# A two-layer graph network on one core: a new order of the opening's tables and loads, and layer-2 scores kept in PSUM

## The chip, the cores and the metric

The program runs on one core of a Trainium2 chip. The metric is the device time of one execution in microseconds (us). The profile names the engines PE (TensorE, matmul), PEld (its weight load), DVE (VectorE), ACT (ScalarE), POOL (GpSimd) and SP (SyncE); DMAs are issued from the queues of SP (SPq), ACT (ACTq) and POOL (POOLq).

## The reference, cut to what matters

There are 12,500 nodes with 64 features and 200,000 edges sorted by destination `dst`; `src` is random.

```python
# layer 1 (batch is all zero, so u[batch] is the row u[0] for every node)
msg = relu(concat([x[dst], x[src], edge_attr_32, u[0]]) @ W1 + b1)
agg = segment_sum(msg, dst)
x1  = layernorm(x + relu(concat([x, agg, u[0]]) @ W2 + b2))
# layer 2: one score per edge, a softmax over the edges of each destination
Z   = einsum('ni,rio->nro', x1, fc_weight)
z_s, z_d = Z[src, etype], Z[dst, etype]
e   = relu(sum(concat([z_s, z_d]) * attn_weight[etype, :, 0]))
m   = segment_max(e, dst);  ex = exp(e - m[dst])
out = layernorm(x1 + segment_sum(ex / segment_sum(ex, dst)[dst] * z_s, dst))
```

## The kernel before

**Edges.** Edges are cut into chunks of 128, four chunks into a run, two runs (8 chunks) into a group: 1563 chunks, 196 groups. Since `dst` is sorted, the destinations of a run fit a window of `W` = 96 nodes. Each layer runs over the groups as a software pipeline: every group is a Python generator (`sum0` in layer 1, `sum1` in layer 2), every tile of 125 nodes another (`finish0`, `finish1`), and the order of the instructions on each engine is the order in which the loops call `group(i)` and `node(i)` under a manual schedule.

**Gathers.** The rows of the sources are fetched by `gather` (L83 to L86), one indirect DMA per chunk, issued by POOL: 8 per group, 1563 per layer. Its offsets lie in SBUF (`src_h`, `src_i`, `row_i`). In layer 1 the rows go to `bg` tiles, of which there are 12, so group g+12 waits until group g's tile has been used. In layer 2 they go to `zg` tiles, of which there are 5.

**The opening.** `W1` splits by its input rows, so the products of all nodes with it are made once: `b_tab` holds x @ W1[sources' rows], `a_tab` holds x @ W1[destinations' rows] plus a common row `c1`. `tables(k)` makes one fifth of both (2500 nodes): 20 matmuls of a 64x125 slice of `xa` (x transposed) against the 64x128 `w1x`, so that sources and destinations come side by side; ACT copies one half to `b_s`, DVE adds `c1` to the other half in `a_s`. SP stores each `b_s` as it is made; ACT stores the five `a_s` after the last. Between the tables DVE makes run data from `dg`: `low` (each run's lowest node), `dr` (destinations less `low`, stored to `rel_tab`), `count`, `at`, and from them the rows `base_row` and `slot_row`, which SP, DVE and ACT read with register loads.

The first `GX` = 6 groups don't wait for `b_tab`: their 48 gathers fetch rows of `x` itself, and PE turns these rows and multiplies them by `w1x` (L385, L395). The gather of group 6 is the first that needs all of `b_tab` and `src_i`. PE begins the first group when `row` has been loaded from `rel_tab`; `row` lies in memory that the opening's tiles leave free, so it also waits for their stores.

**Completion of DMAs.** Direct DMAs of SP and ACT take eight completion semaphores in turn, in program order. A DMA therefore waits at its queue until the one that had its semaphore before it has landed, and what stands behind it in that queue waits too.

**Layer 2.** `psc` is one PSUM bank kept for the whole program. Its first 128 columns hold a row of numbers, `iota`, of which 96 are used; the rest is scratch. `sum1` makes the score `e` of each edge with small DVE instructions (L611 to L617), spreads it over the window by multiplying it with the one-hot `oh` (L625, twice, into `oe` and into `psc`), takes the maxima per node (L627 to L629, then PE and DVE), and goes on to the exponentials on ACT (L674, L676) and the sums on PE (L680). `finish1` normalises the finished nodes; `scale1` scales and stores four tiles at a time, and for each store SP first loads the tile's node number into a register (`n0_of(ENG.SP)`, L724).

```python
for to, i in ((oe, slice(0, half)), (other, slice(half, KS))):
    nc.vector.tensor_mul(to, by_run[:, :, i, :], es[:, :, i].unsqueeze(3).to_broadcast([EC, n, half, W]))
```

Of the kernel before, what the change touches and what calls it, by code (L numbers as in the profile page):

```python
# [29 lines left out]
F32 = mybir.dt.float32  # L30
BF16 = mybir.dt.bfloat16
I32 = mybir.dt.int32
# [7 lines left out]
P = 125  # L40
# [13 lines left out]
NWIN = (N + W - 1) // W  # L54
GX = 6
FIRST = 90
NSL = NG - FIRST
NPT, JT = 5, 20
NQ1 = 4
# [6 lines left out]
def gnn_kernel(ctx: ExitStack, tc, x, xT, src, dstp, dst, et, eaT, u, W1, b1, W2, b2, fc, aw, out):  # L66
# [35 lines left out]
    with (  # L102
# [9 lines left out]
        nc.sync.dma_start(src_h, src[:, :GX * K])  # L112
        dg = pre.tile([NQ, RQ, RE], I32, name="dg")
        nc.sync.dma_start(dg, dst.rearrange("(q r) e -> q r e", r=RQ))
        w1x = consts.tile([D, 2, D], F32, name="w1x")
# [5 lines left out]
        c1 = consts.tile([P, D], F32, name="c1")  # L121
        nc.scalar.dma_start(c1, b1.partition_broadcast(P))
        w2u = consts.tile([DE, D], F32, name="w2u")
        nc.scalar.dma_start(w2u, W2[2 * D:, :])
        c2 = consts.tile([P, D], F32, name="c2")
        nc.scalar.dma_start(c2, b2.partition_broadcast(P))
        w1e = consts.tile([128, D], F32, name="w1e")
        nc.scalar.dma_start(w1e[W:, :], W1[2 * D:2 * D + DE, :])
        for k in range(NPT):
            (nc.scalar if k % 2 else nc.sync).dma_start(xa[:D, part[k]], xT[:, part[k]])  # L130

# [41 lines left out]
        for t in up:  # L173
            nc.vector.memset(t, float(P))
        minus_p = consts.tile([128, 1], F32, name="minus_p")
        nc.vector.tensor_scalar_mul(minus_p, iota_p, -1.0)
        psc = fixed.tile([128, 512], F32, name="psc")

        nc.vector.tensor_copy(psc[:, :128], iota)
        iota_n, iota_r = psc[:EC, :W], psc[:EC, :NR]  # L180


        def common(c, wu):
            ps = pps.tile([P, 4, 2 * D], F32, tag="ab", name="ps_c")
            nc.tensor.matmul(ps[:, 0, :D], u0.to_broadcast([DE, P]), wu, start=True, stop=True)
            nc.vector.tensor_add(c, c, ps[:, 0, :D])

        common(c1, w1u)
        common(c2, w2u)

# [10 lines left out]

        dst_i = keep.tile([EC, NC], I32, name="dst_i")
        a_s = []

        def tables(k):
            b_k = pre.tile([P, JT, D], F32, name="b_s", bufs=3)
            a_k = pre.tile([P, JT, D], F32, name="a_s", bufs=NPT)
            for q in range(JT // 4):
                ps = pps.tile([P, 4, 2 * D], F32, tag="ab", name="ps_ab")
                for i in range(4):  # L210
                    j = k * NP + q * 4 + i
                    nc.tensor.matmul(ps[:, i, :], xa[:D, j:j + JT * (P - 1) + 1:JT], w1x, start=True, stop=True)
                mine = slice(q * 4, q * 4 + 4)
                nc.scalar.copy(b_k[:, mine, :], ps[:, :, D:])
                nc.vector.tensor_add(a_k[:, mine, :], ps[:, :, :D], c1[:, None, :].to_broadcast([P, 4, D]))
            nc.sync.dma_start(b_tab[part[k], :].rearrange("(p j) d -> p j d", j=JT), b_k)
            a_s.append(a_k)
            sums = slice(k * NP, (k + 1) * NP if k < NPT - 1 else N + W)
            nc.scalar.copy(xa[D:, sums], none[D:].to_broadcast([D, sums.stop - sums.start]))

        tables(0)

# [8 lines left out]
        nc.sync.dma_start(bases[1].rearrange("(q r) -> q r", r=RQ), count)  # L231
        tables(1)
        nc.scalar.dma_start(dst_i, dstp)

# [6 lines left out]
        nc.sync.dma_start(bases[2].rearrange("(q r) -> q r", r=RQ), at)  # L241
        tables(2)
        both = pre.tile([1, 3, NRUN], F32, name="both")
        nc.sync.dma_start(both, bases.rearrange("(o s) r -> o s r", o=1))
        tables(3)
        tables(4)
        for k in range(NPT):
            nc.scalar.dma_start(a_tab[part[k], :].rearrange("(p j) d -> p j d", j=JT), a_s[k])
        nc.scalar.dma_start(a_tab[N:, :], zero)


        src_i = keep.tile([EC, NC], I32, name="src_i")
        nc.sync.dma_start(src_i, src)

        aws = []
        for j in range(4):
            t = npool.tile([128, S, D], F32, name=f"aw{j}")
            nc.scalar.copy(t[W:, :, :], w1e[W:, None, :].to_broadcast([DE, S, D]))
            aws.append(t)
        nc.scalar.dma_start(d_tab[N:, :], zero_q)  # L260
        et_i = keep.tile([EC, NC], I32, name="et_i")
        nc.scalar.dma_start(et_i, et)
        w2x = consts.tile([2 * D, D], F32, name="w2x")
        nc.scalar.dma_start(w2x, W2[0:2 * D, :])
        fcw = consts.tile([D, NR, D], F32, name="fcw")
        nc.scalar.dma_start(fcw, fc.rearrange("r i o -> i r o"))
        wsd = consts.tile([D, 2, NR], F32, name="wsd")
        awb = consts.tile([D, 2, NR, D], F32, name="awb")
        for s in range(2):
            nc.scalar.dma_start(awb[:, s, :, :], aw[:, s * D:(s + 1) * D].partition_broadcast(D))  # L270
        rel = keep.tile([EC, NC], F32, name="rel")
# [247 lines left out]
    with (  # L519
# [5 lines left out]
        for i in range(-3, NG + 2):  # L525
# [9 lines left out]
            group(i + 3)  # L535
            if i == 2 * GX:
                later()
# [41 lines left out]

    def sum1(work, psum, n, chunks, idx, rel_of, et_of, row_of, wins_of):  # L580
        row = row_of()
# [34 lines left out]
        nc.vector.tensor_add(e, e, zg[:, :, D])  # L616
        nc.vector.scalar_tensor_tensor(e, e, 0.0, pq[:, :, 3 * NR], OP.max, OP.mult)  # L617


        half = KS // 2  # L620
        by_run, es = oh.rearrange("p (s i) w -> p s i w", s=n), e.rearrange("p (s i) -> p s i", s=n)
        oe = work.tile([EC, n, half, W], F32, name="oe")
# [47 lines left out]
        nc.vector.tensor_reduce(em, pm, AX.X, OP.add)  # L670
        nc.vector.tensor_sub(e, e, em)
        nc.scalar.activation(factor, d, AF.Exp)  # L672
        wz = work.tile([EC, n * KS, C], F32, name="wz")
        nc.scalar.activation(wz[:, :, D], e, AF.Exp)  # L674
        for k in range(n * KS):
# [11 lines left out]

    def finish1(work, psum, n0_of, y_of):

        n0 = n0_of(ENG.SP)  # L690
        xn = work.tile([P, D], F32, name="xn1", bufs=5)
        nc.sync.dma_start(xn, x1_tab[ds(n0, P), :])
        yield
        n0 = n0_of(ENG.Activation)
        own = work.tile([C, P], F32, name="own")
        nc.scalar.copy(own, acc[:, ds(n0, P)])
        yield
        pl = psum.tile([P, C], F32, name="pl")
        nc.tensor.transpose(pl, own, ident[:C, :C])
        yield  # L700
        y, mv = y_of()
        den = work.tile([P, 1], F32, name="den")

        nc.vector.tensor_scalar_max(den, pl[:, D:], 1e-30)
        nc.vector.reciprocal(den, den)
        nc.vector.scalar_tensor_tensor(y, pl[:, :D], den, xn, OP.mult, OP.add)
        st = work.tile([P, nc.vector.BN_STATS_DIM], F32, name="ln_st")
        nc.vector.bn_stats(out=st, in_=y)
        nc.vector.bn_aggr(out=mv, in_=st)

    def scale1(work, n0s_of, y, mv):
        n = len(n0s_of)
        v = work.tile([P, n], F32, name="ln_v")
# [7 lines left out]
        yield  # L721
        for j, n0_of in enumerate(n0s_of):
            nc.scalar.activation(y[:, j, :], y[:, j, :], AF.Identity, bias=shift[:, j:j + 1], scale=v[:, j:j + 1])  # L723
            nc.sync.dma_start(out[ds(n0_of(ENG.SP), P), :], y[:, j, :])  # L724

    with (
# [4 lines left out]
        psum = Banks(pool, pq=2, pb=2)  # L731
        groups, slots, ys, scales = {}, {}, {}, {}

# [7 lines left out]
        for i in range(-3, NG + 4):  # L741
            g = i + 3
            if g < NG:
                n, chunks, c = span(g)
                groups[g] = sum1(work, psum, n, chunks, row_i[:, c], rel[:, c], et_i[:, c],
                                 row_load(work, g), wins_load(g))
            if FIRST <= i < NG:
                slots[i] = finish1(work, psum, slot(i), lambda i=i: y_of(i))
            group(i + 3)
# [26 lines left out]
            if FIRST <= i - 3 < NG and (at == NQ1 - 1 or i - 3 == NG - 1):  # L776
                scales = {q: scale1(work, [slot(j) for j in range(i - 3 - at, i - 2)], *ys[q])}
                next(scales[q])

    with (  # L780
# [11 lines left out]
        def node1(at):  # L792
            y = work.tile([P, 1, D], F32, name="y1")
            mv = work.tile([P, 1, nc.vector.BN_AGGR_DIM], F32, name="ln_mv")
            all_of(finish1(work, psum, lambda engine: at, lambda: (y[:, 0, :], mv[:, 0, :])))
            all_of(scale1(work, [lambda engine: at], y, mv))

# [43 lines left out]
```

## Time and profile before

| | |
|---|---|
| time, median of 3 runs | 4028.84 us (4027.72 to 4029.41) |
| the profiled execution's own time | 4035.53 us |
| its span in the profile | 4033.8 us |
| busy: POOL | 2998.9 us (74%) |
| busy: PE / DVE / ACT | 2966.9 / 2436.6 / 1451.8 us (74 / 60 / 36%) |
| mean granted clock of TensorE | 0.591 |
| first and last gather of layer 1 | 2.88 and 1977.9 us |
| first and last gather of layer 2 | 2002.55 and 3995.6 us |

The span is the time from the first to the last instruction on the chip. A busy share is the time inside instructions; the pause that POOL needs between two gathers is not counted as busy, so POOL's 74% is not a sign of a free quarter. Where an idle stretch stands behind an instruction in square brackets, it gives the time and the event that the profile holds to have ended it.

### The profile page before, as it was taken

The numbers are of one execution on the slowest core, as the hardware profiler recorded it, in microseconds if no ns is written. First come the engines' busy times: TensorE is split into PE (matmuls) and PEld (weight loads), VectorE is DVE, ScalarE is ACT, GpSimd is POOL, SyncE is SP. The second block draws the span as 40 slices with busy tenths as digits, with TensorE's granted clock in tenths as the row PEclk, the third lists the DMA queues.
The fourth block names the chain that finished last, engine by engine and source line by source line (L and its number), as shares of the span: only waits on it lengthen the run. The fifth ranks groups of instructions, "written<-read, shape, count | busy, mean of one in ns | idle before, by whom it ended". The sixth has DMA issues, their size and how long they took to land. (4 is left out here: it accounts for less than half of the span.)

```text
span 4033.8 us, 63353 instructions
## 1 busy us (share of the span) xinstructions
PE 2966.9 (74%) x16445; PEld 2302.5 (57%) x16446; DVE 2436.6 (60%) x8111; ACT 1451.8 (36%) x3714; POOL 2998.9 (74%) x3140
## 2 busy tenths in 40 slices
PE   4977776668999989899666666556666666666664
PEld 4766665557776766667544444444455555555553
DVE  3144433334555555555477777777777787777776
ACT  2100000001111111111265555555556666666665
POOL 5777777777777777777577777777777777777774
PEclk9876655555656565565655556666665555555556
DMA  5222222222333333333221111111122222222221
GB/s 153 50 52 52 51 45 45 45 45 63 77 76 82 78 78 78 78 80 77 63 29 28 28 28 28 28 28 29 29 32 35 35 35 35 35 34 36 34 36 25
DMA packets 292631, 201.38 MB, mean 50 GB/s; under 512 B 213810, under 2 KB 213940, under 8 KB 291841
## 3 DMA queue, kind: packets, MB, share of 16 engines
q0 software_dynamic: 100032, 103.43, 16.2%
q1 hardware_dynamic: 188580, 87.14, 8.6%
q10 hardware_dynamic: 3646, 6.66, 0.6%
q8 instruction: 133, 2.18, 0.2%
q14 instruction: 240, 1.96, 0.2%
HBM read 155.12 MB, written 41.84 MB: 49 GB/s over the span
## 5 line engine op out<-in xcount | busy, mean ns | idle before, releaser
L84 POOL DMA_INDIRECT zg<-z_tab,row_i x1563 | 1518.2, 971 | 499.6 <-issue 422.7
L84 POOL DMA_INDIRECT bg<-b_tab,src_i x1515 | 1430.9, 945 | 482.8 <-issue 425.2
L408 PE MATMUL pa<-oh,msg 128*64 128x96 f32 x3128 | 534.7, 363 | 212.7 <-ACT msg L403 207.9
L403 ACT ACTIVATE msg<-msg 128x512 f32<-128x512 f32 (+1 forms) x190 | 119.4, 629 | 1534.4 <-DVE msg L402 1526.0
L393 PEld LDWEIGHTS pm<-aw,cb 128*128 128x128 f32 x3128 | 558.3, 275 | 128.0 <-issue 123.4
L408 PEld LDWEIGHTS pa<-oh,msg 128*64 128x64 f32 x3128 | 478.4, 221 | 233.5 <-ACT msg L403 223.7
L393 PE MATMUL pm<-aw,cb 128*128 128x64 f32 x3128 | 597.5, 367 | 0.0
L680 PE MATMUL pb<-oh,wz 128*65 128x96 f32 x3128 | 548.4, 368 | 16.6 <-ACT wz L676 4.1
L680 PEld LDWEIGHTS pb<-oh,wz 128*65 128x65 f32 x3128 | 493.9, 227 | 73.3 <-ACT wz L676 73.3
L402 DVE TENSOR_TENSOR msg<-pm,bg 128x512 f32<-128x512 f32 (+1 forms) x190 | 131.1, 690 | 567.7 <-DMA bg<-b_tab,src_i 412.2
L676 ACT ACTIVATE wz<-zg,wz 128x64 f32<-128x64 f32 x1564 | 394.7, 335 | 6.4
L347 DVE TENSOR_TENSOR oh<-psc,rel 128x768 f32<-128x768 f32 x392 | 370.6, 945 | 11.1 <-DMA row<-rel_tab 8.3
L634 PE MATMUL pt<-ident,t 128*96 128x128 f32 x391 | 123.4, 419 | 339.5 <-DVE mq L420 336.5
L594 ACT ACTIVATE off<-ps_row,minus_p 96x512 bf16<-96x512 f32 x391 | 265.8, 680 | 261.6 <-PE ps_row L593 261.6
L593 PE MATMUL ps_row<-row,ones_row 1*96 1x512 bf16 x391 | 209.5, 536 | 192.3 <-ACT off L594 180.0
L414 DVE TENSOR_TENSOR xa<-xa,pa 64x96 f32 x391 | 100.9, 258 | 379.9 <-PE pa L408 372.4
L634 PEld LDWEIGHTS pt<-ident,t 128*96 128x96 f32 x391 | 50.5, 184 | 429.8 <-issue 405.7
L641 PE MATMUL pt<-ident,m 96*65 96x96 f32 x782 | 176.7, 380 | 159.6 <-DVE m L639 159.6
L388 DVE TENSOR_SCALAR cb<-ps_row,iota_p 96x1024 f32<-96x1024 f32 x196 | 246.2, 1256 | 32.2 <-DMA aw<-a_tab 29.9
L641 PEld LDWEIGHTS pt<-ident,m 96*65 96x65 f32 x782 | 119.7, 221 | 176.8 <-DVE m L639 176.8
L341 PE MATMUL ps_row<-row,ones_row 1*96 1x512 bf16 x391 | 183.8, 564 | 39.5 <-DMA fcw<-in_fc 39.5
L597 ACT ACTIVATE ohT<-off 96x1024 bf16<-96x1024 bf16 x196 | 206.6, 1054 | 6.3
(148 smaller groups left out, 3742.7 us busy)
## 6 DMA issues: line engine op xcount, KB each, us to landing
z_tab<-z SPq DMA_DIRECT2D x106, 253.9 KB
zg<-z_tab,row_i POOLq DMA_INDIRECT x1563
cb<-in_eaT SPq DMA_DIRECT2D x195, 128.0 KB
bg<-b_tab,src_i POOLq DMA_INDIRECT x1515
aw<-a_tab SPq DMA_DIRECT2D x391, 24.0 KB
dw<-d_tab SPq DMA_DIRECT2D x391, 4.7 KB
row<-rel_tab SPq DMA_DIRECT2D x390, 2.0 KB
xn<-in_x SPq DMA_DIRECT2D x106, 31.2 KB
```

The lines of the kernel that those rows point to most:

```text
L84: nc.gpsimd.indirect_dma_start(out=to[:, k, :], out_offset=None, in_=table[:, :], in_offset=bass.IndirectOffsetOnAxis(ap=idx[:, k:k + 1], ...
L341: nc.tensor.matmul(ps[:, s, :RE], ones_row, row[:, s, :], start=True, stop=True)
L347: nc.vector.tensor_tensor(oh, iota_n[:, None, :].to_broadcast([EC, n * KS, W]), rel_of.unsqueeze(2).to_broadcast([EC, n * KS, W]), OP.is_e ...
L388: nc.vector.tensor_scalar(cb[:W, :, :], ps_row, iota_p[:W], None, OP.is_equal)
L393: nc.tensor.matmul(pm[:, k, :], cb[:, s, i * EC:(i + 1) * EC], aw_t[:, s, :], start=True, stop=not raw)
L408: nc.tensor.matmul(pa[D:, s, :], msg[:, k, :], oh[:, k, :], start=(i == 0), stop=(i == KS - 1))
L593: nc.tensor.matmul(ps_row[:, :RE], ones_row, row[:, s, :], start=True, stop=True)
L594: nc.scalar.activation(off[:, s, :], ps_row[:, :RE], AF.Abs, bias=minus_p[:W])
L597: nc.scalar.activation(ohT, off, AF.Relu, bias=1.0, scale=-1.0)
L641: nc.tensor.matmul(rows[:, s, :], m[:, s:s + 1].to_broadcast([W, C]), ident[:W, :W], start=True, stop=True)
L676: nc.scalar.activation(wz[:, k, :D], zg[:, k, :D], AF.Copy, scale=wz[:, k, D:])
L680: nc.tensor.matmul(sums[:, s, :], wz[:, k, :], oh[:, k, :], start=(i == 0), stop=(i == KS - 1))
```

## The change

It has four parts.

1. **Scores.** The score of layer 2 is written to 8 columns of `psc` (columns 96 to 111, two places by the group's parity) and no longer to the SBUF tile `e`; the two multiplications of L625 and the subtraction of L671 read it there. `psc` keeps 96 columns of `iota` instead of 128.
2. **Opening.** `tables` is split: `sources(k)` for all five parts first, each 20 matmuls against the 64 source columns of `w1x`, then `destinations(k)` for all five. A PSUM tile now holds five products of 64 columns instead of four of 128. All stores of both tables are issued on SP, each as its part is made. `b_s` has 5 buffers and `a_s` 3. The parts of `xa` are loaded before the weights of `W2`, `w1e`, `dst_i` and `src_i`, which go to SP's queue; parts 0, 1 and 3 come on ACT's queue and 2 and 4 on SP's. `dst_i` and `src_i` are loaded ahead of the tables. The zero rows of `a_tab` and `d_tab` are stored early. `xa`'s lower half is cleared in one instruction at the end. The loads of `et_i`, `w2x`, `fcw` and `awb` are issued by ACT one per round of layer 1's loop, from round 2 on, and `later()`, which uses them, runs in round 20 instead of 12.
3. **Groups of x.** `GX` is 5: 40 gathers fetch rows of `x`, and the gather of group 5 is the first that needs `b_tab`.
4. **Stores of the result.** SP keeps each tile's node number in a register from `finish1` on, and `scale1` uses it, so the 106 register loads of L724 are gone.

```diff
-GX = 6
+GX = 5
-NPT, JT = 5, 20
+NPT, JT, JQ = 5, 20, 5
...
+        dg = pre.tile([NQ, RQ, RE], I32, name="dg")
+        nc.sync.dma_start(dg, dst.rearrange("(q r) e -> q r e", r=RQ))
+        for k in range(NPT):
+            (nc.sync if k in (2, 4) else nc.scalar).dma_start(xa[:D, part[k]], xT[:, part[k]])
         w2u = consts.tile([DE, D], F32, name="w2u")
-        nc.scalar.dma_start(w2u, W2[2 * D:, :])
+        nc.sync.dma_start(w2u, W2[2 * D:, :])
...
-        for k in range(NPT):
-            (nc.scalar if k % 2 else nc.sync).dma_start(xa[:D, part[k]], xT[:, part[k]])
+        nc.sync.dma_start(dst_i, dstp)
+        src_i = keep.tile([EC, NC], I32, name="src_i")
+        nc.sync.dma_start(src_i, src)
...
+        nc.sync.dma_start(a_tab[N:, :], zero)
+        nc.sync.dma_start(d_tab[N:, :], zero_q)
...
-        nc.vector.tensor_copy(psc[:, :128], iota)
+        nc.vector.tensor_copy(psc[:, :W], iota[:, :W])
...
-        def tables(k):
...
+        def products(k, side):
+            for q in range(JT // JQ):
+                ps = pps.tile([P, JQ, D], F32, tag="ab", name="ps_ab")
+                for i in range(JQ):
+                    j = k * NP + q * JQ + i
+                    nc.tensor.matmul(ps[:, i, :], xa[:D, j:j + JT * (P - 1) + 1:JT], w1x[:, side, :],
+                                     start=True, stop=True)
+                yield slice(q * JQ, (q + 1) * JQ), ps
+
+        def sources(k):
+            b_k = pre.tile([P, JT, D], F32, name="b_s", bufs=NPT)
+            for mine, ps in products(k, 1):
+                nc.scalar.copy(b_k[:, mine, :], ps)
             nc.sync.dma_start(b_tab[part[k], :].rearrange("(p j) d -> p j d", j=JT), b_k)
...
+        def destinations(k):
+            a_k = pre.tile([P, JT, D], F32, name="a_s", bufs=3)
+            for mine, ps in products(k, 0):
+                nc.vector.tensor_add(a_k[:, mine, :], ps, c1[:, None, :].to_broadcast([P, JQ, D]))
+            nc.sync.dma_start(a_tab[part[k], :].rearrange("(p j) d -> p j d", j=JT), a_k)
+
+        for k in range(NPT):
+            sources(k)
...
-        tables(1)
-        nc.scalar.dma_start(dst_i, dstp)
+        destinations(0)
...
-        for k in range(NPT):
-            nc.scalar.dma_start(a_tab[part[k], :].rearrange("(p j) d -> p j d", j=JT), a_s[k])
-        nc.scalar.dma_start(a_tab[N:, :], zero)
+        for k in range(2, NPT):
+            destinations(k)
+        common(c2, w2u)
+        nc.scalar.copy(xa[D:, :], none[D:].to_broadcast([D, N + W]))
...
-            if i == 2 * GX:
+            if i >= 2 and loads:
+                nc.scalar.dma_start(*loads.pop(0))
+            if i == 20:
                 later()
...
-        nc.vector.scalar_tensor_tensor(e, e, 0.0, pq[:, :, 3 * NR], OP.max, OP.mult)
+        score = psc[:EC, W + odd * K:W + odd * K + n * KS]
+        nc.vector.scalar_tensor_tensor(score, e, 0.0, pq[:, :, 3 * NR], OP.max, OP.mult)
...
-        by_run, es = oh.rearrange("p (s i) w -> p s i w", s=n), e.rearrange("p (s i) -> p s i", s=n)
+        by_run, es = oh.rearrange("p (s i) w -> p s i w", s=n), score.rearrange("p (s i) -> p s i", s=n)
...
-        nc.vector.tensor_sub(e, e, em)
+        nc.vector.tensor_sub(em, score, em)
...
-            nc.sync.dma_start(out[ds(n0_of(ENG.SP), P), :], y[:, j, :])
+            nc.sync.dma_start(out[ds(n0, P), :], y[:, j, :])
```

More of the change, by code (lines that the diff above doesn't have):

```diff
@@ L112, in gnn_kernel @@
         nc.sync.dma_start(src_h, src[:, :GX * K])
-        dg = pre.tile([NQ, RQ, RE], I32, name="dg")
-        nc.sync.dma_start(dg, dst.rearrange("(q r) e -> q r e", r=RQ))
         w1x = consts.tile([D, 2, D], F32, name="w1x")
@@ L122, in gnn_kernel @@
         nc.scalar.dma_start(c1, b1.partition_broadcast(P))
+        dg = pre.tile([NQ, RQ, RE], I32, name="dg")
+        nc.sync.dma_start(dg, dst.rearrange("(q r) e -> q r e", r=RQ))
+        for k in range(NPT):
+            (nc.sync if k in (2, 4) else nc.scalar).dma_start(xa[:D, part[k]], xT[:, part[k]])
         w2u = consts.tile([DE, D], F32, name="w2u")
-        nc.scalar.dma_start(w2u, W2[2 * D:, :])
+        nc.sync.dma_start(w2u, W2[2 * D:, :])
         c2 = consts.tile([P, D], F32, name="c2")
-        nc.scalar.dma_start(c2, b2.partition_broadcast(P))
+        nc.sync.dma_start(c2, b2.partition_broadcast(P))
         w1e = consts.tile([128, D], F32, name="w1e")
-        nc.scalar.dma_start(w1e[W:, :], W1[2 * D:2 * D + DE, :])
-        for k in range(NPT):
-            (nc.scalar if k % 2 else nc.sync).dma_start(xa[:D, part[k]], xT[:, part[k]])
+        nc.sync.dma_start(w1e[W:, :], W1[2 * D:2 * D + DE, :])
+        dst_i = keep.tile([EC, NC], I32, name="dst_i")
+        nc.sync.dma_start(dst_i, dstp)
+        src_i = keep.tile([EC, NC], I32, name="src_i")
+        nc.sync.dma_start(src_i, src)
         ident = consts.tile([128, 128], F32, name="ident")
@@ L177, in gnn_kernel @@
         psc = fixed.tile([128, 512], F32, name="psc")
-        nc.vector.tensor_copy(psc[:, :128], iota)
+        nc.vector.tensor_copy(psc[:, :W], iota[:, :W])
         iota_n, iota_r = psc[:EC, :W], psc[:EC, :NR]
         def common(c, wu):
-            ps = pps.tile([P, 4, 2 * D], F32, tag="ab", name="ps_c")
-            nc.tensor.matmul(ps[:, 0, :D], u0.to_broadcast([DE, P]), wu, start=True, stop=True)
-            nc.vector.tensor_add(c, c, ps[:, 0, :D])
+            ps = pps.tile([P, JQ, D], F32, tag="ab", name="ps_c")
+            nc.tensor.matmul(ps[:, 0, :], u0.to_broadcast([DE, P]), wu, start=True, stop=True)
+            nc.vector.tensor_add(c, c, ps[:, 0, :])
         common(c1, w1u)
-        common(c2, w2u)
         low = pre.tile([NQ, RQ], F32, name="low")
@@ L199, in gnn_kernel @@
         nc.sync.dma_start(rel_tab.rearrange("(q r) e -> q r e", r=RQ), dr)
-        dst_i = keep.tile([EC, NC], I32, name="dst_i")
-        a_s = []
-        def tables(k):
[L206 to L215, printed above, removed]
-            nc.sync.dma_start(b_tab[part[k], :].rearrange("(p j) d -> p j d", j=JT), b_k)
[L217 to L221, printed above, removed]
+        def products(k, side):
[10 more added lines that the diff above has]
+                nc.scalar.copy(b_k[:, mine, :], ps)
+            nc.sync.dma_start(b_tab[part[k], :].rearrange("(p j) d -> p j d", j=JT), b_k)
+        def destinations(k):
[5 more added lines that the diff above has]
+            sources(k)
         high = pre.tile([NQ, RQ], F32, name="high")
@@ L241, in gnn_kernel @@
         nc.sync.dma_start(bases[2].rearrange("(q r) -> q r", r=RQ), at)
-        tables(2)
+        destinations(1)
         both = pre.tile([1, 3, NRUN], F32, name="both")
         nc.sync.dma_start(both, bases.rearrange("(o s) r -> o s r", o=1))
-        tables(3)
-        tables(4)
-        for k in range(NPT):
-            nc.scalar.dma_start(a_tab[part[k], :].rearrange("(p j) d -> p j d", j=JT), a_s[k])
-        nc.scalar.dma_start(a_tab[N:, :], zero)
-        src_i = keep.tile([EC, NC], I32, name="src_i")
-        nc.sync.dma_start(src_i, src)
+        for k in range(2, NPT):
+            destinations(k)
+        common(c2, w2u)
+        nc.scalar.copy(xa[D:, :], none[D:].to_broadcast([D, N + W]))
         aws = []
@@ L259, in gnn_kernel @@
             aws.append(t)
-        nc.scalar.dma_start(d_tab[N:, :], zero_q)
         et_i = keep.tile([EC, NC], I32, name="et_i")
-        nc.scalar.dma_start(et_i, et)
         w2x = consts.tile([2 * D, D], F32, name="w2x")
-        nc.scalar.dma_start(w2x, W2[0:2 * D, :])
         fcw = consts.tile([D, NR, D], F32, name="fcw")
-        nc.scalar.dma_start(fcw, fc.rearrange("r i o -> i r o"))
         wsd = consts.tile([D, 2, NR], F32, name="wsd")
         awb = consts.tile([D, 2, NR, D], F32, name="awb")
-        for s in range(2):
-            nc.scalar.dma_start(awb[:, s, :, :], aw[:, s * D:(s + 1) * D].partition_broadcast(D))
+        loads = [(et_i, et), (w2x, W2[0:2 * D, :]), (fcw, fc.rearrange("r i o -> i r o"))]
+        loads += [(awb[:, s, :, :], aw[:, s * D:(s + 1) * D].partition_broadcast(D)) for s in range(2)]
         rel = keep.tile([EC, NC], F32, name="rel")
@@ L578, in gnn_kernel, with sum1 @@
         nc.scalar.copy(t, none[:C].to_broadcast([C, N + W]))
-    def sum1(work, psum, n, chunks, idx, rel_of, et_of, row_of, wins_of):
+    def sum1(work, psum, n, chunks, idx, rel_of, et_of, row_of, wins_of, odd=0):
         row = row_of()
@@ L670, in sum1 @@
         nc.vector.tensor_reduce(em, pm, AX.X, OP.add)
-        nc.vector.tensor_sub(e, e, em)
+        nc.vector.tensor_sub(em, score, em)
         nc.scalar.activation(factor, d, AF.Exp)
         wz = work.tile([EC, n * KS, C], F32, name="wz")
-        nc.scalar.activation(wz[:, :, D], e, AF.Exp)
+        nc.scalar.activation(wz[:, :, D], em, AF.Exp)
         for k in range(n * KS):
@@ L685, in sum1, with finish1 @@
             nc.vector.tensor_add(mine, mine, sums[:, s, :])
-    def finish1(work, psum, n0_of, y_of):
+    def finish1(work, psum, n0_of, y_of, tell=lambda n0: None):
         n0 = n0_of(ENG.SP)
@@ L692, in finish1 @@
         nc.sync.dma_start(xn, x1_tab[ds(n0, P), :])
+        tell(n0)
         yield
@@ L709, in finish1, with scale1 @@
         nc.vector.bn_aggr(out=mv, in_=st)
-    def scale1(work, n0s_of, y, mv):
-        n = len(n0s_of)
+    def scale1(work, n0s, y, mv):
+        n = len(n0s)
         v = work.tile([P, n], F32, name="ln_v")
@@ L721, in scale1 @@
         yield
-        for j, n0_of in enumerate(n0s_of):
+        for j, n0 in enumerate(n0s):
             nc.scalar.activation(y[:, j, :], y[:, j, :], AF.Identity, bias=shift[:, j:j + 1], scale=v[:, j:j + 1])
-            nc.sync.dma_start(out[ds(n0_of(ENG.SP), P), :], y[:, j, :])
+            nc.sync.dma_start(out[ds(n0, P), :], y[:, j, :])
     with (
@@ L731, in gnn_kernel @@
         psum = Banks(pool, pq=2, pb=2)
-        groups, slots, ys, scales = {}, {}, {}, {}
+        groups, slots, ys, scales, places = {}, {}, {}, {}, {}
         def y_of(i):
@@ L745, in gnn_kernel @@
                 groups[g] = sum1(work, psum, n, chunks, row_i[:, c], rel[:, c], et_i[:, c],
-                                 row_load(work, g), wins_load(g))
+                                 row_load(work, g), wins_load(g), g % 2)
             if FIRST <= i < NG:
-                slots[i] = finish1(work, psum, slot(i), lambda i=i: y_of(i))
+                slots[i] = finish1(work, psum, slot(i), lambda i=i: y_of(i), lambda n0, i=i: places.update({i: n0}))
             group(i + 3)
@@ L776, in gnn_kernel @@
             if FIRST <= i - 3 < NG and (at == NQ1 - 1 or i - 3 == NG - 1):
-                scales = {q: scale1(work, [slot(j) for j in range(i - 3 - at, i - 2)], *ys[q])}
+                scales = {q: scale1(work, [places[j] for j in range(i - 3 - at, i - 2)], *ys[q])}
                 next(scales[q])
@@ L795, in node1 @@
             all_of(finish1(work, psum, lambda engine: at, lambda: (y[:, 0, :], mv[:, 0, :])))
-            all_of(scale1(work, [lambda engine: at], y, mv))
+            all_of(scale1(work, [at], y, mv))
         leftover(more1, node1)
```

## Prediction

> **What bounds the kernel now.** I read the page's busy row first, then POOL's groups and its waits, because POOL's idle time is where a kernel of 3126 gathers shows its limit:
>
> ```profile
> PE 2966.9 (74%) x16445; PEld 2302.5 (57%) x16446; DVE 2436.6 (60%) x8111; ACT 1451.8 (36%) x3714; POOL 2998.9 (74%) x3140
> L84 POOL DMA_INDIRECT zg<-z_tab,row_i x1563 | 1518.2, 971 | 499.6 <-issue 422.7 <-DVE t L628 26.2 <-DMA zg<-z_tab,row_i 22.9
> L84 POOL DMA_INDIRECT bg<-b_tab,src_i x1515 | 1430.9, 945 | 482.8 <-issue 425.2 <-DMA a_tab<-zero 21.4 <-DMA bg<-b_tab,src_i 18.6
> L84 POOL DMA_INDIRECT bg<-in_x,src_h x48 | 47.9, 999 | 15.0 <-issue 14.3 <-DMA src_h<-in_src 0.7
> ```
>
> Busy and idle of the three groups add up to 1518.2 + 499.6 + 1430.9 + 482.8 + 47.9 + 15.0 = 3994.4 us of the 4033.8. POOL is never free: between two gathers it pauses 0.30 us, whatever the name behind the arrow. Two idle stretches alone are longer, one of 21.38 us ahead of the first gather of `b_tab` and one of 23.5 us between the layers. So the time is 3126 gathers of about 0.944 + 0.304 = 1.248 us (3901), plus these two stretches (44), plus gathers that take longer than usual (46), plus 2.9 us ahead and 37 us behind. Only the last four can change.
>
> The tile view and the timeline show the longer gathers: median 944 ns, maximum 1332, and who runs when one starts late:
>
> ```profile
> L84 POOL DMA_INDIRECT zg<-z_tab,row_i x1563: 940/944/1332, 2002.5 to 3995.6; - x196
> 3984.36 0.17 DVE L616 TENSOR_TENSOR e<-e,zg 128x8 f32<-128x8 f32 x1 [1.48 <-DMA zg<-z_tab,row_i]
> 3984.76 0.56 DVE L625 TENSOR_TENSOR oe<-oh,e 128x384 f32<-128x384 f32 x1
> 3985.24 0.56 DVE L625 TENSOR_TENSOR psc<-oh,e 128x384 f32<-128x384 f32 x1
> 3985.42 1.19 POOL L84 DMA_INDIRECT zg<-z_tab,row_i  x1 [0.31 <-issue]
> ```
>
> The opening, and the end, from the timeline:
>
> ```profile
> 11.72 2.29 DVE L198 TENSOR_TENSOR dr<-dg,low 98x2048 bf16<-98x2048 int32 x1
> 11.77 3.06 POOL L84 DMA_INDIRECT bg<-in_x,src_h  x1 [0.30 <-issue]
> 19.17 46.61 PE L212 MATMUL ps_ab<-w1x,xa 64*125 64x128 f32 x200 [9.94 <-DMA xa<-in_xT]
> 25.56 0.36 SPq L196 DMA_DIRECT2D base_b<-bases  x1
> 66.21 10.76 ACTq L248 DMA_DIRECT2D a_tab<-a_s  x4
> 86.52 0.94 POOL L84 DMA_INDIRECT bg<-b_tab,src_i  x1 [21.38 <-DMA a_tab<-zero]
> 105.31 1.05 PE L341 MATMUL ps_row<-row,ones_row 1*96 1x512 bf16 x2 [39.53 <-DMA fcw<-in_fc]
> 4017.08 9.62 SPq L724 DMA_DIRECT2D out<-y  x6
> 4021.08 0.75 ACT L723 ACTIVATE y<-y,ln_shift,ln_v 125x64 f32<-125x64 f32 x2
> ```
>
> The reader is to see that the gather at 86.5 doesn't really wait for `a_tab`: its inputs are `b_tab` and `src_i`, and the last `b_s` store (issued at 66.2) runs beside the `a_tab` stores. In windows, the stores run at 130 GB/s from 30 to 35 us with one queue storing, and at 124 GB/s from 70 to 84 with two: the second queue adds nothing.
>
> **Part 1, scores: -39 us.** The excess of `zg` gathers over 944 ns sums to 1518.2 - 1563 x 0.944 = 42.7 us. Counted over the trace by what DVE runs in a gather's first 250 ns, 194 gathers of `zg` meet L625, and they take 217 ns more on average: 42.2 us. Beside other DVE instructions the excess is nil: 380 gathers meet L347 (one input in PSUM, one in SBUF, 945 ns long), 176 L629, 150 L402, with means within 1 ns of 944. L650 (both inputs in SBUF, 250 ns) adds 6 ns on average. L198 above, both inputs in SBUF, holds a gather for 2.1 us. So what holds a gather is a running DVE instruction with both inputs in SBUF. After the change L625 has `oh` in SBUF and the score in PSUM, like L347.
>
> [...] L649 with one input in PSUM takes 0.24 us, L650 of the same shape with none 0.25. Either way it is covered: DVE waits 253.8 us in 180 groups at L616 for the gather (1.4 us each)[...].
>
> What is late next: gathers after L625 come 0.22 us earlier against DVE's chain, which starts anew at each L616. Shifted by that, about a third of the 390 L650 start within 50 ns of a gather's start, where the trace shows holds of 0 to 54 ns. I count 3 us (bounds 0 and 390 x 83 ns, the longest hold seen at L650, = 32). Sum -42 + 3 = -39.
>
> **Part 2 and 3, the opening: -10 us.** PE: 200 half products of 64 columns instead of 100 of 128. The row above is 233 ns per pass, two passes a matmul; at 64 columns the pair L393 and L395 takes 0.615 us from 115 to 123 us, so 0.31 a matmul and 31 us for each table. Loads move 208 GB/s from 2 to 24 us. Ahead of the tables now stand `dg`, `xa` and 1.6 MB of `dst_i` and `src_i`: 5.6 MB, done by about 30. `xa`'s first part lands at 11 to 16, not 19, so the sources are done at 44 to 48.
>
> But SP's queue is in order. `low` waits for the last part of `xa`, then lands behind `src_i` in the same queue, at about 31.5 (before, landing took from 11.7 to 25.6 behind three parts of `xa`). `base_b` waits for it, and behind `base_b` stand `rel_tab` and all five `b_s` stores. So these start at about 35, and take 625 KB at 115 GB/s (the 130 above less the gathers' 15 to 20) = 5.7 us each: the last lands at about 63 to 64 (bounds 57, if `low` lands at 26, and 68). 40 gathers of x end at 54, so POOL waits about 9.5 us instead of 21.4: a gain of 12, all bounds 7 to 18.
>
> Two things take some back. DVE's `rel` (L272, 1.78 us) and the minima of L304 and L312 (15 short instructions with two SBUF inputs) ran while POOL stood still; now they run at 75 to 91, beside gathers: +2 to 3 us by the hold above. And `bg` has 12 buffers. The gather of group 17 needs group 5 used. The `a_s` stores follow the `b_s` stores in one queue, to 64 + 5 x 5.7 = 92; then `row` and PE start at about 96 (before 105.3). Before, group 6 was used 98.9 us after PE's start, with six groups of x of 11 to 16 us; with five that is 85 to 91, at 181 to 187. POOL comes to group 17 at 63.5 + 12 x 9.98 = 183. This is on the edge (before, the margin was 2.1 us at group 18), worth 0 to 4 us, and partly the same microseconds as the hold. Sum -12 + 2 = -10.
>
> Costed at nothing: the clearing of `xa` in one piece (some 11 us on ACT, covered by the destinations' 31 us on PE), `c2`, and the ACT loads in the loop (ACT is 1 to 2 tenths busy there; a late one would delay `later()`, not needed until group 90). The stretch of 23.5 us between the layers stays: what ends it is the chain behind the last gather.
>
> **Part 4, stores: -4 us.** Inside the loop SP is no bound. At the end it is: the last ACT result is there at 4021.83, but SP, at 1.7 us a store with a register load of 0.53 us and a wait, issues its sixth store at 4026.4, and everything to 4033.8 follows that. Without the loads it follows ACT at about 4022.2: -4 (bounds -1, -5).
>
> **Sum.** -39 - 10 - 4 = -53 on the profiled 4035.53 us gives 3982.5; that execution stood 6.7 above the median of 4028.84, so 3976.
>
> **The rivals.**
> 1. *As above*, 3976 (own range 3968 to 3986), 74%.
> 2. *PE gives it back*: stores run slower in one queue, or PE's slow stretch falls on the groups of x, and POOL stands at group 17 for the 10 us gained and up to 10 more: 3986 to 3996. For it: the margin of 2.1. Against: the 130 GB/s of one queue. 12%.
> 3. *`low` does not get stuck* and the stall vanishes: the whole 21.4, so 3965. Against: the 13.9 us that it was stuck before. 7%.
> 4. *The hold stays*[...]: -10 - 4, so 4015. 4%.
> 5. *Slower*: the hold comes from L625's length[...], and PSUM makes each of the two longer[...]. [...] It decides as soon as a hold grows by over 0.07 us. Against: L649 and L347. 3%.
>
> **The numbers.** Rivals 1 to 4 end over 0.2% (8 us) below 4028.84, which is about what a measurement of this kernel can tell from no change; rival 5 above it. With 1% in between: faster 0.96, same 0.01, slower 0.03. The range 3964 to 3994 takes in rivals 1 and 3 and most of 2.
>
> **What would show it.** POOL's mean for `zg` falls from 971 to 944 to 950 ns; the gather of `b_tab` starts near 64 with a wait of 5 to 14 us ahead of it; PE's first `ps_row` is near 96; a second POOL wait of under 5 us stands near 183; the last store of `out` is issued near the last ACT result. I am wrong if `zg` stays above 960, if the b_tab wait is over 17 us, or if POOL waits over 10 us at group 17.

## The result

The changed kernel takes 4007.29 us (median of 5 runs, 4000.85 to 4011.78) against 4028.84 (5 runs, 4027.72 to 4029.99): a ratio of 0.9946, 95% interval 0.9932 to 0.9961. It is faster by 21.5 us. Forecast were 53 us, and 4007 lies outside the range of 3964 to 3994. The profiled execution took 4007.29 us with a span of 4005.4.

The groups of POOL in the profile after (busy, mean of one, idle before):

```profile
L84 POOL DMA_INDIRECT zg<-z_tab,row_i x1563 | 1477.4, 945 | 499.4 <-issue 414.7 <-DMA zg<-z_tab,row_i 41.2 <-ACT top L657 23.2
L84 POOL DMA_INDIRECT bg<-b_tab,src_i x1523 | 1442.1, 947 | 492.2 <-issue 443.2 <-DMA bg<-b_tab,src_i 23.5 <-DVE msg L405 13.0
L84 POOL DMA_INDIRECT bg<-in_x,src_h x40 | 39.3, 982 | 15.7 <-issue 11.3 <-DMA bg<-in_x,src_h 3.7 <-DMA src_h<-in_src 0.7
```

The tile view (shortest, median and longest gather, first and last start):

```profile
L84 POOL DMA_INDIRECT zg<-z_tab,row_i x1563: 940/945/1028, 2015.0 to 3967.5; - x196
```

Layer 2, from its first to its last gather, fell from 1993.1 to 1952.5 us: -40.6, as forecast (-39). But its first gather starts at 2015.0, not at 2002.5: the opening, forecast to win 10, lost 12.4. And from the last gather to the end are 37.9 us where there were 38.2: -0.3, forecast -4. Together that is the difference of the two spans (4033.8 to 4005.4). The medians differ by less, 21.5, because the profiled execution of the kernel before stood 6.7 above its median and this one does not (its 4007.29 is the median).

The opening in the timeline after, PE, the stores on SP's queue, and POOL:

```profile
18.96 92.17 PE L213 MATMUL ps_ab<-w1x,xa 64*125 64x64 f32 x400 [7.74 <-DMA xa<-in_xT]
30.87 0.34 SPq L202 DMA_DIRECT2D base_b<-bases  x1
31.77 34.12 SPq L221 DMA_DIRECT2D b_tab<-b_s  x5
73.38 0.94 POOL L84 DMA_INDIRECT bg<-b_tab,src_i  x1 [16.19 <-issue]
93.30 18.64 SPq L227 DMA_DIRECT2D a_tab<-a_s  x3
123.47 1.05 PE L344 MATMUL ps_row<-row,ones_row 1*96 1x512 bf16 x2 [11.74 <-issue]
207.07 0.94 POOL L84 DMA_INDIRECT bg<-b_tab,src_i  x1 [12.37 <-DVE msg L405]
```

Nearly the whole loss is seen here. The tables keep PE busy for 92 us, twice as long as before (46.61). `x400` counts two records for each of the 200 fp32 matmuls; each record is called a pass below. So the sources are done at 65, `b_tab` at 73, the destinations at 111, and PE starts its first group at 123.5 where it started at 105.3. POOL stands twice, 16.19 and 12.37 us, where it stood once for 21.38. That is +7.2 of the 12.4. Gathers of `x` that wait for earlier ones (3.7 us in the row of `in_x`, of which some 3 are more than the usual pauses; before, no such wait is listed) and gathers that last longer (the busy time of layer 1's gathers is 1481.4 us, before 1478.8) are the rest.

### The profile page after: what moved, and what is told of

Its sections match the earlier page's. It is cut to its first block, busy times and chain, and to the rows that moved or that the text cites. A ratio compares the mean times of both kernels' runs of the same rounds, so it can differ in the third digit from the quotient of the medians.

```text
span 4005.4 us, 63587 instructions
## 1 busy us (share of the span) xinstructions
PE 2987.8 (75%) x16621; PEld 2323.1 (58%) x16622; DVE 2472.5 (62%) x8107; ACT 1447.4 (36%) x3703; POOL 2960.7 (74%) x3140
## 5 line engine op out<-in xcount | busy, mean ns | idle before, releaser
L84 POOL DMA_INDIRECT zg<-z_tab,row_i x1563 | 1477.4, 945 | 499.4 <-issue 414.7
L406 ACT ACTIVATE msg<-msg 128x512 f32<-128x512 f32 x191 | 120.0, 628 | 1548.6 <-DVE msg L405 1531.7
L396 PEld LDWEIGHTS pm<-aw,cb 128*128 128x128 f32 x3128 | 548.8, 271 | 126.4 <-issue 122.6
L396 PE MATMUL pm<-aw,cb 128*128 128x64 f32 x3128 | 586.8, 362 | 0.0
L405 DVE TENSOR_TENSOR msg<-pm,bg 128x512 f32<-128x512 f32 x191 | 131.7, 690 | 579.5 <-DMA bg<-b_tab,src_i 432.8
```

The lines of the kernel that those rows point to most:

```text
L84: nc.gpsimd.indirect_dma_start(out=to[:, k, :], out_offset=None, in_=table[:, :], in_offset=bass.IndirectOffsetOnAxis(ap=idx[:, k:k + 1], ...
L396: nc.tensor.matmul(pm[:, k, :], cb[:, s, i * EC:(i + 1) * EC], aw_t[:, s, :], start=True, stop=not raw)
```

## The experiments

| kernel | us | ratio to the kernel before | 95% interval |
|---|---|---|---|
| changed kernel | 4007.3 | 0.9946 | 0.9932 to 0.9961 |
| e1, scores and stores | 4000.1 | 0.9922 | 0.9905 to 0.9938 |
| e1c, scores | 3994.0 | 0.9897 | 0.9882 to 0.9912 |
| e2, opening and 5 groups of x | 4044.0 | 1.0026 | 1.0015 to 1.0038 |
| e3, weights side by side | 4003.9 | 0.9923 | 0.9907 to 0.9940 |
| e4, 16 buffers of `bg` | 3998.5 | 0.9917 | 0.9900 to 0.9933 |
| v2b, tables of 128 columns | 3993.0 | 0.9892 | 0.9877 to 0.9907 |
| e5b, 6 groups of x, 16 buffers | 3980.8 | 0.9861 | 0.9846 to 0.9876 |
| v1b, 128 columns, 7 groups, 16 buffers | 3976.1 | 0.9851 | 0.9837 to 0.9864 |

The runs were made on several chips, so ratios are compared, not times (the kernel before took 4031.6 us beside e1 to e4 and 4036.1 beside e1c, v2b, e5b and v1b). Even ratios carry some 10 us from one chip to the next: e1c, v2b, e5b and v1b, all on one chip, each came out about 10 us below what e1 or the changed kernel on other chips led to expect. Differences of that size are therefore read within one chip, or from the traces. e0, e7, e8 and e9 are single executions. The kernels of v2b, v1b and e5b also ran on one more chip, on which they took 5398 to 5468 us and the kernel before 5478 to 5523, with POOL idle over 1000 us longer than elsewhere. The ratios there were 0.9835, 0.9854 and 0.9900. Why that chip is slower is not known, and nothing else is drawn from it.

### e1 and e2: the change in two halves

e1 is the kernel before with parts 1 and 4, e2 the kernel before with parts 2 and 3.

> The kernel before with part 1 (scores in PSUM) and part 4 (no register load at a store) alone: old opening, six groups of x, tables of 128 columns. Theory A (the changed kernel loses in the opening what it should have won there: first layer-2 gather 2014.9 against 2002.6): the hold of the zg gathers goes as in the changed kernel, -41 us, and the opening stays, so 4028.8 - 41 = 3988, faster than the changed kernel's 4007. The mean zg gather is 945 ns, the first b_tab gather starts at 86.5 again. Rival B (the split in the trace is an accident, the opening is worth 0 or the 10 us that the prediction gave it, and the scores are worth only 20 on the median): 4007 or above. Part 4 is expected to be worth 0 by what the changed kernel's trace shows, -4 by the prediction.

> The kernel before with parts 2 and 3 alone (new opening, five groups of x); scores in SBUF and register loads as before. Theory A: +12 by the first layer-2 gather of the changed kernel, so 4041; the first b_tab gather is near 73 and POOL stands about 12 us at group 17. Rival B, the prediction's step for this part: -10, so 4019. The mean zg gather stays at 971 ns in both.

Measured: e1 is 31.5 us faster than the kernel before, e2 12.4 us slower (4044.03 against 4031.64). The scores win and the opening loses; the sum, -19, is near the changed kernel's -21.5. POOL stands at group 17 for 17.3 us in e2. The hold, the extra length of `zg` gathers, remains there, but is smaller:

```profile
L84 POOL DMA_INDIRECT zg<-z_tab,row_i x1563 | 1509.4, 966 | 500.5 <-issue 422.1 <-DMA zg<-z_tab,row_i 51.5 <-ACT own L701 16.5
```

Its gathers sum to 29 us over their median of 947 ns, where the kernel before has 43 over 944, though e2's layer 2 is that of the kernel before. About as many gathers meet the two multiplications of the scores (202 against 203, counting every overlap in a gather's first 250 ns), and each is held for less on average (148 ns against 208). What the hold costs depends also on where in the pair of multiplications a gather starts: in the kernel before, 110 gathers that started 0.6 to 0.7 us after the pair's start were held for 251 ns on average, 17 at 0.7 to 0.8 us for 180. So e2's +12.4 has a gain of this kind in it. Its opening alone lost more: the first layer-2 gather starts at 2022.0, where the kernel before has 2002.5. e1's trace has `b_tab`'s first gather at 86.0, after the old wait of 21.4.

### e1c: the scores alone

```diff
-        nc.vector.scalar_tensor_tensor(e, e, 0.0, pq[:, :, 3 * NR], OP.max, OP.mult)
+        score = psc[:EC, W + odd * K:W + odd * K + n * KS]
+        nc.vector.scalar_tensor_tensor(score, e, 0.0, pq[:, :, 3 * NR], OP.max, OP.mult)
...
```

> The kernel before with part 1, the scores, alone. By the excess of the zg gathers in the two traces (42.7 us before, 1.9 after): -41, ratio 0.990. By the times of the run with scores and stores: -31.5, ratio 0.992. If it is the latter, 8 to 10 us of the traced gain come back elsewhere in the execution. Stores are expected to be worth 0, so this is also the time of scores and stores together.

Measured: -42.1 us, 0.9897. This is the -41 of the traces. The -31.5 of e1 lies outside e1c's interval; the two intervals meet at 0.9905 to 0.9912, a gain of 36 to 38 us. One thing differs in the traces: in those of e1 to e4 the usual gather took 947 ns, in that of e1c 944. For 3126 gathers 3 ns are 9 us. Whether the kernel before shared them beside e1 is not known, so the 10 us between e1 and e1c stay open. Another profile of the kernel before (e0) has 944 ns, a `zg` mean of 970 and a span of 4033.0 again. On e0's own chip e7, e8 and e9 had 947 ns, while v2b, v1b and e5b had 944 like e1c, so the chip alone does not set it; what does was not shown.

> The kernel before, profiled once more, since its first profiled execution stood 6.7 us above the median of its runs and the changed kernel's did not. Expected: span 4027 to 4034, first b_tab gather at 86 to 87 with a wait of 21.4 us, first layer-2 gather at 2002 to 2004, mean zg gather 971 ns. If the zg mean is nearer 965, the hold was worth about 31 us in this kernel's ordinary runs and not 42.

### e7 and e8: what holds a gather

Each adds one DVE multiplication to every layer-2 group of the changed kernel, after L635, as long as one of the two of the scores.

```diff
e7 +        nc.vector.tensor_mul(probe, oh[:, :, :48], zg[:, :, :48])
e8 +        nc.vector.tensor_mul(probe, oh[:, :, :48], iota_n[:, None, :48].to_broadcast([EC, n * KS, 48]))
```

> The changed kernel with one more DVE multiplication in each layer-2 group (128x384, as long as one of the two of the scores), both inputs in SBUF; its result isn't used. Theory P (a running DVE instruction with two SBUF inputs holds a gather that starts beside it): some gathers are held again by 0.2 us and more, up to one per group; the mean zg gather rises from 945 to 950 to 970 ns, the layer by 10 to 40 us. Rival T (what the score had done before was not a matter of the inputs' place): 945 ns, no change.

> The same added multiplication with its second input in PSUM (the row of numbers iota_n). Theory P: the mean zg gather stays at 945 to 946 ns and the time at the changed kernel's 4007 (within its own spread of 4001 to 4012). Rival T: the same rise as with both inputs in SBUF, if there was one.

The tile view of `zg`, first e7, then e8:

```profile
L84 POOL DMA_INDIRECT zg<-z_tab,row_i x1563: 941/947/1320, 2020.1 to 3978.1; - x196
```

```profile
L84 POOL DMA_INDIRECT zg<-z_tab,row_i x1563: 941/947/1025, 2019.4 to 3973.6; - x196
```

and the added groups on DVE, again e7, then e8:

```profile
L637 DVE TENSOR_TENSOR probe<-oh,zg 128x384 f32<-128x384 f32 x196 | 107.9, 551 | 0.0
```

```profile
L637 DVE TENSOR_TENSOR probe<-oh,psc 128x384 f32<-128x384 f32 x196 | 107.0, 546 | 0.0
```

The two instructions take the same time; only with both inputs in SBUF does a gather stretch to 1320 ns. Counted over the traces, 52 gathers of e7 had the probe running within their first 250 ns, took 66 ns more than the median on average, and 12 of them over 80 more; in e8 about 50 met it, at -1 ns on average, and none took 80 more. So it is the place of the inputs, not the length of the instruction. (e7's second input is `zg` itself, which gathers write; in the kernel before, neither input of L625 was, and the hold was there.) The size was over-expected: the layer grew by 3.8 us (1958.0 against 1954.3 from first to last gather), not by 10 to 40, because at this place of the chain only 52 gathers of 1563 meet the probe and were held by 66 ns, where in the kernel before 194 met the scores' pair and were held by 217. The executions took 4018.6 and 4014.3 us; e8's lies above the expected 4001 to 4012, with the first layer-2 gather 4.4 us later than in the changed kernel (2019.4 against 2015.0) and a usual gather of 947 ns against 945.

### e4: where the wait at group 17 comes from

```diff
-    bpool = nodes.enter_context(tc.tile_pool(name="sources", bufs=12))
+    bpool = nodes.enter_context(tc.tile_pool(name="sources", bufs=16))
```

> The changed kernel with 16 buffers of bg instead of 12, so that POOL may run four groups further ahead of PE in layer 1. Theory A (the wait of 12.4 us at group 17 comes from PE's late start and from nothing else): the wait goes, the first b_tab gather stays at 73, the time is 4007 - 12 = 3995. Rival C (PE in layer 1 is slow enough after its late start that POOL only meets the same wait some groups later, at group 21): the wait moves to group 21 and shrinks little, 4003 to 4007.

Waits of POOL for `msg` (us in total, times, longest), in the changed kernel, then in e4:

```profile
POOL bg L84 <- DVE msg L405: 13.0, 3, 12.4
```

```profile
POOL bg L84 <- DVE msg L405: 0.6, 2, 0.3
```

PE starts at 123.56, as in the changed kernel (123.47), and no later group waits: with 16 buffers the late start costs nothing. Theory A holds by the trace. The ratio, 0.9917 against 0.9946, is about 12 us lower, but it compares two chips.

### e3 and e9: what a pass of the tables costs

```diff
-                    j = k * NP + q * JQ + i
-                    nc.tensor.matmul(ps[:, i, :], xa[:D, j:j + JT * (P - 1) + 1:JT], w1x[:, side, :],
+                    j = k * NP + (q * JQ + i) * P
+                    nc.tensor.matmul(ps[:, i, :], xa[:D, j:j + P], w1x[:, side, :],
```

> The changed kernel, but the 125 columns of xa that each matmul of the two tables loads as weights stand side by side and not 20 apart. The rows of both tables come out in another order within each fifth, so the messages of layer 1 are those of other nodes; the number and size of all instructions is the same. Theory S (a load of weights at a stride of 80 bytes sets the 0.229 us per pass, which is why 64 columns take as long as 128): a matmul of the tables falls from 0.46 to about 0.31 us, the 200 of them from 92 to about 62 us, b_tab's first gather moves from 73 to about 64 to 68, PE's first group starts at 100 to 110 and not 133, the 12 us at group 17 go, and the time is about 3985 to 3990. Rival F (the 0.229 is a fixed price of a pass with 64x125 fp32 weights, whatever their stride): no change, 4007, 0.46 us a matmul.

Measured in e3's timeline:

```profile
18.37 84.23 PE L213 MATMUL ps_ab<-w1x,xa 64*125 64x64 f32 x400 [7.57 <-DMA xa<-in_xT]
115.02 1.05 PE L344 MATMUL ps_row<-row,ones_row 1*96 1x512 bf16 x2 [11.81 <-issue]
```

84.2 us instead of 92.2: the stride (the distance between the columns taken) is worth 9%, where theory S forecast a third; theory S fell, and F's "no change" is nearer. The first gather of `b_tab` came at 68.9 instead of 73.4, so the work of PE sets its time. POOL still stood 11.2 us at group 17, and the ratio of 0.9923 is not clearly apart from the changed kernel's.

e9 takes the weights in ten ways, one a part. The diff shows how; the first number of each pair is the step between columns, the second their count.

```diff
+        ways = {(1, 0): (20, 125), (1, 1): (1, 125), (1, 2): (1, 128), (1, 3): (19, 128), (1, 4): (2, 125),
+                (0, 0): (1, 128), (0, 1): (4, 125), (0, 2): (19, 125), (0, 3): (19, 128), (0, 4): (1, 125)}
...
```

> The changed kernel with ten ways of taking the weights of the tables' matmuls, one for each part: sources 0 to 4 with 125 columns 20 apart (as in the changed kernel), 125 side by side, 128 side by side, 128 columns 19 apart, 125 columns 2 apart; destinations 0 to 4 with 128 side by side, 125 columns 4 apart, 125 columns 19 apart, 128 columns 19 apart, and 125 side by side of 32 rows. The tables then hold other nodes' rows. Each part's time is read from the start of its PSUM copies, 40 passes each. Theory C (125 columns in place of 128 make a load of weights slow): the three 128-column parts take 0.154 us per pass as L396 and L398 do (6.2 us a part), the 125-column parts 0.21 to 0.23. Theory R [...]: all parts stay at 0.21 to 0.23. Theory S (stride costs the rest): parts of step 1 at 0.21, step 2 and 4 between, 19 and 20 at 0.23, whatever the number of columns.

ACT (DVE for the destinations) copies each PSUM tile when its five matmuls, ten passes, are done, so the distance of two starts is ten passes. Here for sources 0 (20 apart, 125), 1 (side by side, 125) and 2 (side by side, 128):

```profile
24.00 0.43 ACT L225 COPY b_s<-ps_ab 125x320 f32<-125x320 f32 x1 [1.87 <-PE ps_ab L218]
26.29 0.43 ACT L225 COPY b_s<-ps_ab 125x320 f32<-125x320 f32 x1 [1.87 <-PE ps_ab L218]
...
32.81 0.43 ACT L225 COPY b_s<-ps_ab 125x320 f32<-125x320 f32 x1 [1.67 <-PE ps_ab L218]
34.91 0.43 ACT L225 COPY b_s<-ps_ab 125x320 f32<-125x320 f32 x1 [1.67 <-PE ps_ab L218]
...
41.29 0.43 ACT L225 COPY b_s<-ps_ab 125x320 f32<-125x320 f32 x1 [1.71 <-PE ps_ab L218]
43.42 0.43 ACT L225 COPY b_s<-ps_ab 125x320 f32<-125x320 f32 x1 [1.71 <-PE ps_ab L218]
```

That is 2.29, 2.10 and 2.13 us. Over all ten: 2.10 to 2.14 for columns side by side or 2 apart (125 or 128 of them, of 64 rows or of 32), 2.24 to 2.32 for columns 4, 19 and 20 apart. A pass costs 0.21 to 0.23 us in all of them, and 0.233 with 128 moving columns (those of `w1x`, the matmul's other operand) in the kernel before. Among these ways the number of passes sets the time, and the step between columns changes it by 9%. So theory R is right in what it says of the time, S in that a larger step costs the rest, and C falls. (C's 0.154 us per pass was a misreading: L396 and L398 take 0.31, see below.) How the load of weights and the running matmul share a pass was not tried.

### v2b: the split undone

100 matmuls of 128 columns make both halves again; `b_s` is stored first and `a_s` after it, on SP, as in the changed kernel.

```diff
-                    nc.tensor.matmul(ps[:, i, :], xa[:D, j:j + JT * (P - 1) + 1:JT], w1x[:, side, :],
-                                     start=True, stop=True)
+                    nc.tensor.matmul(ps[:, i, :], xa[:D, j:j + JT * (P - 1) + 1:JT], w1x, start=True, stop=True)
...
```

> The changed kernel with the split of the tables undone: 100 matmuls of 128 columns make both halves again; the order of loads, the one queue with b_s first and a_s after it, five groups of x and the scores stay. Theory R (a pass costs 0.21 to 0.23 us whatever its columns, so the split doubles PE's work in the opening): tables done at 66 instead of 111, b_tab's first gather stays at 71 to 74 since the sources are done at 65 either way, the a_s stores end near 100, PE's first group starts at 106 to 110 and not 123.5, group 5 is used at about 200 to 204, so the 12.4 us at group 17 shrink to 0 to 3: a ratio to the kernel before of about 0.992 (the changed kernel has 0.9946). Rival Q (PE's late start comes from the single queue of stores): PE starts at 120 or later, no gain.

The timeline of v2b:

```profile
19.36 46.66 PE L217 MATMUL ps_ab<-w1x,xa 64*125 64x128 f32 x200 [7.78 <-DMA xa<-in_xT]
75.17 0.94 POOL L84 DMA_INDIRECT bg<-b_tab,src_i  x1 [18.65 <-issue]
104.30 1.05 PE L342 MATMUL ps_row<-row,ones_row 1*96 1x512 bf16 x2 [37.68 <-DMA row<-rel_tab]
```

PE starts 19 us earlier, in spite of the single queue, and group 17 does not wait: theory R against rival Q. `b_tab` comes at 75, no earlier than with the split. The ratio, expected at 0.992, is 0.9892. Against e1c's 0.9897 on the same chip it says what parts 2, 3 and 4 together are worth without the split: nothing that these runs can tell.

### e5b and v1b: room for POOL

e5b is the changed kernel with `GX` 6 and 16 buffers of `bg`; v1b is v2b with `GX` 7 and 16 buffers.

> The changed kernel with six groups of x and 16 buffers of bg, split tables kept. Theory R: the wait ahead of b_tab falls from 16.2 to about 6, group 22 finds its buffer free, 22 us less than the changed kernel, ratio 0.989: the split then costs only what b_tab is late, and PE's start at 123 to 134 costs nothing. Rival W (PE's late start is felt in any case): a wait of over 5 us at group 22, ratio 0.9905 or more.

> The version that the runs point to: the changed kernel with tables of 128 columns, seven groups of x (gathers of x until 77, past the landing of b_tab at 72) and 16 buffers of bg. Theory R: no wait ahead of the first b_tab gather (16.2 us in the changed kernel) and none at a later group (12.4): 28 us less than the changed kernel, ratio 0.9875 to 0.988. Rival W (more groups of x delay PE, and POOL waits for buffers at group 23): a wait of 5 to 15 us there, ratio 0.989 to 0.9915.

POOL at the first gather of `b_tab`, in e5b, then in v1b:

```profile
66.18 0.94 POOL L84 DMA_INDIRECT bg<-in_x,src_h  x1 [0.30 <-issue]
74.30 0.94 POOL L84 DMA_INDIRECT bg<-b_tab,src_i  x1 [7.18 <-issue]
```

```profile
78.29 0.94 POOL L84 DMA_INDIRECT bg<-in_x,src_h  x1 [0.30 <-issue]
79.54 0.94 POOL L84 DMA_INDIRECT bg<-b_tab,src_i  x1 [0.31 <-issue]
```

In v1b no wait of POOL in layer 1 is longer than 0.7 us apart from gathers of `x` that wait 2.4 for earlier ones. It is 60 us faster than the kernel before and the fastest of all. Both came out about 10 us better than expected, from a ratio that was measured on another chip. The split costs e5b next to nothing: it is 4.7 us slower than v1b (the two intervals overlap), and has a wait of 7.18 left that v1b's seventh group of `x` covers. No later group of e5b waits for a buffer, so a late PE is harmless once POOL has enough of them.

## Why the prediction was wrong

**What bounds it:** right. In all kernels of the table POOL's gathers set the time (3126 of 0.944 to 0.947 us, each with its pause of 0.30, are about 3900 of the 3976 to 4044 us), and the gains are its waits and its long gathers.

**Part 1, -39:** right in mechanism, and near in size. The excess of the `zg` gathers over 944 ns fell from 42.7 to 1.9 us, layer 2 by 40.6, the time of e1c by 42, but that of e1 by 31.5, and e2 shows the hold itself at 29. The 3 us given to L650 were not seen. The PSUM source cost nothing that shows: the pair of multiplications takes 552 and 561 ns, before 557 and 559, and the added one 546 in e8 against 551 in e7. That a PSUM source makes such an instruction longer, as rival 5 had it, was not shown. e7 and e8 show the hold's cause on an added instruction: 66 ns on average with both inputs in SBUF, -1 with one in PSUM.

**Parts 2 and 3, -10:** the step that failed is "at 64 columns the pair L393 and L395 takes 0.615 us from 115 to 123 us, so 0.31 a matmul and 31 us for each table". It was a misreading. The timeline of the kernel before there:

```profile
114.19 0.69 PE L395 MATMUL pm<-w1x,bT 64*128 64x64 f32 x2
114.80 0.69 PE L393 MATMUL pm<-aw,cb 128*128 128x64 f32 x2
115.42 0.69 PE L395 MATMUL pm<-w1x,bT 64*128 64x64 f32 x2
```

Each row, `x2`, is the two passes of one fp32 matmul, and rows follow each other by 0.615: that is 0.615 a matmul, 0.31 a *pass*, and a pair takes 1.23. Read rightly, the rows give no sign that 64 columns are cheaper than the 0.233 us a pass of the 128-column tables. At that price the 400 passes of the split take PE 93 us instead of 46.6. They took 92.2, 46 a table instead of 31.

The loads of weights of the tables, before and after, between 20 and 110 us:

```profile
L212 PEld LDWEIGHTS ps_ab<-w1x,xa 64*125 64x125 f32 x197 | 45.7, 325 | 0.0
L213 PEld LDWEIGHTS ps_ab<-w1x,xa 64*125 64x125 f32 x393 | 90.4, 323 | 0.0
```

Twice as many loads keep the weight side busy twice as long, and one of them lasts as long as before, although it serves half the moving columns. These records, 323 ns long, overlap: a pass comes every 210 to 230.

What follows from this step came as the chain of the prediction has it, only later. `xa`'s first part landed at 18.9, no sooner than before (forecast 11 to 16), so PE could not begin earlier. `base_b` was issued at 30.87 (forecast about 31.5). SP's queue kept its order: `rel_tab`, whose `dr` was done at 20.13, left right behind it at 31.31, and the store of `count`, done at 24.06, left at 65.94 behind the last of `b_s`. On its way SP also waited 4.6 us at `w1e` for `c` and 3.2 us at `dst_i` for a part of `xa`, which had the completion semaphores that these two take. But the last `b_s` store was issued at 65.6, PE being the limit and not the queue, so `b_tab` came at 73.4 instead of 63 to 64. The destinations' tables and their stores put PE's first group at 123.5 instead of 96. Group 5 was used 83 us after that (forecast 85 to 91, near), and POOL stood at group 17 for 12.4 instead of 0 to 4, over the 10 that the prediction had named as proof against itself. Rival 2, with its wait at group 17, had the place right; its price was for a kernel whose `b_tab` came at 64. With PE's work halved again (v2b), the wait at group 17 goes; `b_tab` still comes at 75, so the -12 was not there for the wide tables either.

Term by term, the opening's -12 for `b_tab` became -5.2 (21.38 to 16.19), and its 0 to 4 at group 17 became 12.4. The waits among the gathers of `x`, some 3 us, were not in the forecast. The longer gathers cost 2.6 (forecast 2 to 3; about 1.6 of it is the usual gather's 945 ns instead of 944). `b_tab` did come 13 us sooner (86.5 to 73.4), but the choice of five groups of `x`, made for a `b_tab` at 64, gave 8 gathers or 10 us of cover away: with six, e5b waits 7.18.

**Part 4, -4:** wrong. SP's wait for the earlier store hid the register load. SP's waits before, then after (us, times, longest):

```profile
SPq L724 <- DMA out<-y: 61.7, 80, 1.8
```

```profile
SPq L731 <- DMA out<-y: 103.3, 80, 2.3
```

80 waits grew by 0.52 us each, just the 0.53 us of the load that is gone. The last ACT result comes at 3993.8, and the last six stores still take from 3989.1 to 3998.3. The tail, from the last gather to the end, is 37.8 us in e1 with the change and 38.2 in e1c without it; over all traces of the table it is 37.7 to 39.1 with it and 37.8 to 38.2 without.

## What to carry to other kernels

Before a product is split, count its passes: here a pass cost 0.23 us with 64 moving columns as with 128, so two halves took twice the time (92.2 us against 46.6). A row with a count may hold passes, not instructions: check its pace against a group whose number of matmuls is known from the code. And when an engine behind the bound starts late, look at the buffers between the two first: 16 instead of 12 made the lateness free (0.6 us of waits for `msg` instead of 13.0).

## What was not expected of the hardware

A pass of fp32 weights took 0.21 us with columns side by side or 2 apart and 0.23 with columns 4 to 20 apart. 125 or 128 columns made no difference, nor did 32 or 64 rows, nor 64 or (before) 128 moving columns. L393 and L395, of 128 columns, took 0.31 a pass at the same full clock (granted clock 1.00 from 113 to 140 us); why was not tried. The changed kernel's runs spread over 11 us, and e3's, with a wait of 11.2 us at group 17, over 12. With that wait gone (e4, v2b) the spread was 3 and 2. But e2, which stood 17.3 us there, spread over 5, and the kernel before over 2, 4 and 5 on three chips. The wait ends with PE's work on the groups of `x`, in a stretch in which the granted clock falls (0.86 from 140 to 180 us, 0.50 from 180 to 220 in the changed kernel). That this makes the spread is argued, and these runs don't show it.
